# A transformer block on one core: the last product of the first attention moves into the second attention, some copies change their issuing queue, and the last output product is computed transposed

## The chip, the cores and the metric

The kernel runs on one core of a Trainium2 chip. TensorE multiplies matrices and transposes by multiplying with an identity, VectorE and ScalarE work element by element, GpSimd (POOL in the profile) does elementwise work and gathers, and SyncE (SP) does nothing but issue transfers. Every engine works through its own instructions in the order in which they were written; semaphores order work between engines. The metric is the device time of one execution in microseconds, as the median of three runs.

## The reference

The input `x` has 8 batches of 128 rows and 512 columns, all in float32. The block computes

```
h   = einsum('bsi,boi->bso', x, L0_cond_weight[itok_B_3_7])
x   = x + attention_1(h) @ wo          # 32 heads of 16, causal, 8 key/value heads
a   = attention_2(x) @ Wo              # 32 heads of 128, 8 key/value heads, rmsnorm and rotation
                                       # of q and k, 512 cached keys per batch plus 128 own
out = x + ffn(a)                       # a @ kernel + bias + two low-rank products
```

In the second attention the product with `Wo` is a sum over the 8 key/value heads (each with 4 query heads), so the kernel may add up one head after the other.

## The kernel before, in words

The order of the instructions on each engine is the order in which the Python code emits them. There is no planner: `tc.manual_schedule()` keeps it.

**First part, 0 to about 241 us.** A loop over `k` runs through 16 half batches of the conditioned projection and the first attention. For each batch `out_proj1(b)` multiplies the attention's output `oT[b]` by `wo_sb` (eight passes of 128x512 on TensorE, L650), adds the loaded rows of `x` on VectorE (L654) and stores the sum as `x1_kept[b]` (L655). `flip_x1(b)` transposes that sum (four transposes, L483) and ScalarE copies it to `x1T[b]` (L659), which the second attention reads. For the last batch both calls stand after the loop, around `own_keys(0)` and the last two `merge_w` (L468), so that the first scores of the second attention follow them on TensorE. Weights for the second attention are loaded during the loop, the ones of the output product by `load_wo(0)` and `load_wo(1)` (L135).

**Second part, about 241 to 1421 us.** `units` lists 64 pairs (head group `g`, batch `b`), with the two heads of a pair next to each other; a cached block holds both heads' keys. The loop over `u` is a software pipeline. Step `u` computes the scores and the softmax of unit `u`, the projections of unit `u + 1` (`q_matmul` L175, `kv_matmul` L215, `kv_turn`, `norms`, `queries` L252, `own_keys` L271), and the values and the output product of unit `u - 1` (`values` L894, `out_proj` L913). TensorE's order in a step is: scores with the next unit's q products between them, k and v products, values of the last unit, transposes of the next unit's q, output product of the last unit, transpose of the next unit's keys (kTp).

Within `scores`, VectorE masks and scales each of four score tiles (L851), ScalarE takes the exponential (L861) and later divides by the sum (L829), whose reciprocal VectorE makes (L828). VectorE transposes the four tiles in 32x32 blocks into `flips` (L832). Then 16 copies of 80 KB put the blocks in place as `pT` (L882), all issued by SyncE:

```
for a in range(4):
    for k in range(4):
        nc.sync.dma_start(out=s["pT"][32 * k : 32 * k + 32, a]..., in_=s["flips"][32 * a : 32 * a + 32, k]...)
```

Cached keys are turned in the same way, for two units at once: `turn_keys(n)` transposes blocks on VectorE into `flk` (L789) and `move_keys(n, a)` issues four copies each for `a` = 0 to 3 (L802). For most pairs eight of these fall into each step. The first such pair, n = 1, has to do all sixteen in step 1, and they stand in `pair_keys`, which `scores` calls after the third tile, ahead of the fourth exponential. The keys of units 0 and 1 are transposed by TensorE instead (`keys`, L263).

GpSimd adds the two halves of the rotation (L201), computes the power -1/2 for the norms (L242), and then gathers the cached rows (L158).

**The end.** Batch `b` is finished when its unit of the last head group has been added to `y_acc[b]` (L920). One step later `ffn_flip(b)` transposes it (L926) and ScalarE copies it as `yT` (L928); `ffn_lora(b)` makes a small product (axp, L945) which ScalarE copies to `ax`; `ffn(b)` makes the large products (fp, L960 and L961), adds the residual on VectorE (L963) and stores. In step 63 this is done for batch 6: flip, values of unit 62, axp, output product of unit 62, fp. Step 64 has only the values and the output product of unit 63, and step 65 the FFN of batch 7.

Of the kernel before, what the change touches and what calls it, by code (L numbers as in the profile page):

```python
# [41 lines left out]
def block_kernel(  # L42
# [75 lines left out]
    x1_kept = [dram.tile([P, DM], F32, tag=f"x1_{b}", name=f"x1_kept_{b}") for b in range(B)]  # L118
    b_kept = dram.tile([B, RANK, DM], F32, tag="b_eff", name="b_kept")
    res = {}  # L120

    weights = {}

# [8 lines left out]
    def load_wo(g):  # L132
        wo = wpool.tile([P, REP, DM], F32, tag="wo", name=f"wo_{g}")
        e = slice(g * REP * D2, (g + 1) * REP * D2)
        nc.sync.dma_start(out=wo[:], in_=wo2[e, :].rearrange("(r p) o -> p r o", p=P))  # L135
        weights[g].append(wo)
# [139 lines left out]
    with (  # L276
# [3 lines left out]
        wq_sb = p1w.tile([P, KC, REP * P], F32, tag="wq_sb", name="wq_sb")  # L280
        wk_sb = p1w.tile([P, KC, P], F32, tag="wk_sb", name="wk_sb")
        wv_sb = p1w.tile([P, KC, P], F32, tag="wv_sb", name="wv_sb")
        wo_sb = p1w.tile([P, REP, DM], F32, tag="wo_sb", name="wo_sb")
        xss, cws = {}, {}

        def load_x(b):
# [339 lines left out]
        def values1(k):  # L626
            b, hb = divmod(k, 2)
            h = H[k]
            if hb == 0:
                oT[b] = p1.tile([P, REP, S], F32, tag="oT1", name=f"oT1_{b}")  # L630
            ps = p_mm.tile([P, 2 * S], F32, tag="mm", name=f"o1_{k}")
            for half in range(2):
                for j in range(4):
                    nc.tensor.matmul(  # L634
                        ps[32 * j : 32 * j + 32, :],
                        vpad[b % 2][:, j, half].rearrange("p s d -> p (s d)"),
                        h[f"pT_{j}"][:, half, :],
                        start=(half == 0),
                        stop=(half == 1),
                    )  # L640
            nc.vector.tensor_copy(
                oT[b][:, 2 * hb : 2 * hb + 2, :].rearrange("p r t -> p (r t)"), ps[:]
            )
# [13 lines left out]
        def flip_x1(b):  # L657
            tp = transposed(x1[b], f"x1Tp_{b}")
            nc.scalar.copy(x1T[b][:], tp[:])  # L659
# [13 lines left out]
        for k in range(2 * B + 1):  # L673
            b, hb = divmod(k, 2)
            more, now, last = b + 1 < B, k < 2 * B, k - 1
            if now:
                scores1(k)
            if hb == 0:
                if b >= 2:
                    flip_x1(b - 2)  # L680
                if now:
                    exps1(k, 0)
                if more:
                    condition(b + 1)
                if k == 2 * B - 2:
                    for i in range(KC):
                        merge_a(i)
                if now:
                    exps1(k, 1)
                if k == 2 * B:  # L690
                    queries(0)
                if k:
                    flip_p(last, 0, by_vector)
                    flip_p(last, 1, by_vector)
                if now:
                    divide1(k, 0)
                    divide1(k, 1)
                if more:
                    kv = project_kv(b + 1)
                if k == 2 * B:  # L700
                    merge_b(0)
                if k:
                    flip_p(last, 2, by_scalar)
                    flip_p(last, 3, by_scalar)
                if more:
                    keep_k(b + 1, kv)
                if k == 2 * B:
                    merge_b(1)
                    for i in range(2):
                        merge_w(i)  # L710
                if k:
                    values1(last)
                if more:
                    keep_v(b + 1, kv)
                gather_w(b + 3)
                if k == 2 * B - 4:
                    merge_gates()
            else:
                if b >= 1:
                    out_proj1(b - 1)  # L720
                exps1(k, 0)
                exps1(k, 1)
                flip_p(last, 0, by_vector)
                flip_p(last, 1, by_vector)
                divide1(k, 0)
                divide1(k, 1)
                if more:
                    ps = project_q(b + 1)
                    keep_q(b + 1, ps)
                else:  # L730
                    for c in range(KC):
                        q_matmul(0, c)
                    for part in q_turn(0):
                        part()
                    for c in range(KC):
                        kv_matmul(0, c)
                flip_p(last, 2, by_scalar)
                flip_p(last, 3, by_vector)
                if not more:
                    kv_turn(0)  # L740
                    norms(0)
                if b + 2 < B:
                    flip_x(b + 2)
                values1(last)
                load_x(b + 4)
                if b == 0:
                    indices()
                elif b == 1:
                    tables(0)
                    load_qkv(0)  # L750
                    load_wo(0)
                elif b == 2:
                    tables(1)
                    nc.gpsimd.memset(minus_half[:], -0.5)
                elif b == 3:
                    load_qkv(1)
                    load_wo(1)
                elif b == B - 2:
                    gather(0, "kg")
                    gather(0, "vg")  # L760
                if b == 4:
                    merge_loads()
        keys(0)
        out_proj1(B - 1)
        own_keys(0)
        for i in range(2, KC):
            merge_w(i)
        flip_x1(B - 1)


    p2c = ctx.enter_context(tc.tile_pool(name="p2c", bufs=1))
# [7 lines left out]
    nc.gpsimd.memset(place[:, NBLK * P :], -3.0e38)  # L779

    y_acc = [p2c.tile([P, DM], F32, tag=f"y_{b}", name=f"y_{b}") for b in range(B)]

    def turn_keys(n):

# [13 lines left out]

    def move_keys(n, a):

        for b in range(4):
            nc.sync.dma_start(  # L802
                out=pairs[n]["kT"][32 * b : 32 * b + 32, :, a].rearrange("p c m i -> p c (m i)"),
                in_=pairs[n]["flk"][32 * a : 32 * a + 32, b].rearrange("p c m i -> p c (m i)"),
            )
# [9 lines left out]
    def scores(u, between, after):  # L815
# [62 lines left out]

        s["pT"] = p2.tile([P, 4, NBLK + 1, REP, 32], F32, tag="pT2", name=f"pT_{u}")
        for a in range(4):  # L880
            for k in range(4):
                nc.sync.dma_start(  # L882
                    out=s["pT"][32 * k : 32 * k + 32, a].rearrange("i c r j -> i (c r j)"),
                    in_=s["flips"][32 * a : 32 * a + 32, k].rearrange("i c r j -> i (c r j)"),
                )
# [21 lines left out]
    def out_proj(u, r):  # L907
        g, b = units[u]
        s = st[u]
        if r == 0:  # L910
            s["yp"] = p_mm.tile([P, DM], F32, tag="mm", name=f"yp_{u}")
        yp = s["yp"]
        nc.tensor.matmul(  # L913
            yp[:], s["oT"][:, r, :], weights[g][2][:, r, :], start=(r == 0), stop=(r == REP - 1)
        )
        if r == REP - 1:
            if g == 0:
                nc.scalar.copy(y_acc[b][:], yp[:])
            else:
                nc.vector.tensor_tensor(y_acc[b][:], yp[:], y_acc[b][:], ALU.add)  # L920


    def ffn_flip(b):
        tp = p_tp.tile([P, KC, S], F32, tag="tp", name=f"yTp_{b}")
        for c in range(KC):
            nc.tensor.transpose(tp[:, c, :], y_acc[b][:, c * P : (c + 1) * P], ident[:])  # L926
        yT = tile_a([P, KC, S], f"yT_{b}")
        nc.scalar.copy(yT[:], tp[:])  # L928
        return yT
# [35 lines left out]

    pending = []
    first = (NKV // 2 - 1) * 2 * B
    for u in range(N + 3):


        now, nxt, last = u < N, u + 1 < N, 1 <= u <= N
# [11 lines left out]
        if nxt:  # L983
# [2 lines left out]
            kv_turn(u + 1)  # L986
            after[1]()
        flipped = [(b, ffn_flip(b)) for b in pending]
        if last:
            values(u - 1)  # L990
        if nxt:
            norms(u + 1)
            queries(u + 1)
            keys(u + 1)
            if u > 2 and u % 2 and u // 2 + 2 < N // 2:
                turn_keys(u // 2 + 2)

            if u < 2:
                gather(u + 1, "kg")
            elif u % 2 == 0:  # L1000
                gather(u // 2 + 2, "kg")
            if u % 2:
                gather(u // 2 + 1, "vg")
        flipped = [(b, yT, ffn_lora(b, yT)) for b, yT in flipped]
        if last:
            for r in range(REP):
                out_proj(u - 1, r)
        if nxt:
            own_keys(u + 1)

        for n in range(2):
            g = (u + 1 - n) // (2 * B) * 2 + 2 + n
# [8 lines left out]
                ffn_loads(b + 1)  # L1021
        if u == first:
            ffn_loads(0)
        pending = [units[u - 1][1]] if last and units[u - 1][0] == NKV - 1 else []


# [76 lines left out]
```

## Time and profile before

| | |
|---|---|
| median of three runs | 1442.05 us (1441.12 to 1443.71) |
| the profiled execution, its own time | 1443.16 us |
| its span, first to last instruction | 1441.4 us |
| TensorE busy in the span | 1404.8 us (97%) |
| VectorE, ScalarE, GpSimd busy | 932.7 us, 652.6 us, 564.3 us |
| mean granted TensorE clock | 0.996 |
| SyncE's copies of pT, of kT | 1024 of 80 KB, 496 of 32 KB |

The profile shows one execution. PE stands for TensorE's multiplications, PEld for its weight loads, DVE for VectorE, ACT for ScalarE, POOL for GpSimd, SP for SyncE; a q after the name is the engine's sequencer, where transfers are issued. A name such as `pT<-fl` says which tile is written from which. In the timeline a line gives start and length in us, engine, source line, operation, shapes and count, and in brackets how long the engine was idle before and what ended the wait. Times count from the start of the span. A matmul of float32 appears as two passes, each with its own record.

### The profile page before, as it was taken

Reading aid. Unit: us, or ns where it says so; the run is one execution under the profiler, and the core shown is the slowest. Engines: PE = TensorE matmul, PEld = TensorE weight load, DVE = VectorE, ACT = ScalarE, POOL = GpSimd, SP = SyncE. Lnnn points to the kernel's source line nnn. Section 1 sums busy time; section 2 is a strip of 40 time slices with the busy share of each in tenths; the row PEclk is TensorE's granted clock in tenths of the full one; section 3 lists DMA queues with packets and bytes.
Section 4 is the critical chain, followed back from the end, with each engine's and each line's share of the span. In section 5 each row is a group of like instructions: output and inputs, shape, how many; then the busy total and the mean of one; then the engine's idle time right before and its main releaser. Section 6 shows DMA issues by size and latency. Waiting matters only on the chain.

```text
span 1441.4 us, 19823 instructions
## 1 busy us (share of the span) xinstructions
PE 1404.8 (97%) x5984; PEld 897.3 (62%) x6000; DVE 932.7 (65%) x2271; ACT 652.6 (45%) x1513; POOL 564.3 (39%) x546
## 2 busy tenths in 40 slices
PE   6999999899999999999999999999999999999997
PEld 5677764566666666666666666666666665666554
DVE  4666674666666666666666666666666665666652
ACT  3454543444444444444444444444444444344430
POOL 4675242433333333333433344444343333343220
PEclk9999999999999999999999999999999999999999
DMA  5233410444444575444445654444457544444442
GB/s 202 75 117 120 142 44 23 134 120 118 117 117 117 150 191 159 118 117 117 118 119 160 194 149 119 119 119 119 119 161 193 157 125 136 123 115 114 112 111 66
DMA packets 159770, 181.82 MB, mean 126 GB/s; under 512 B 94960, under 2 KB 100336, under 8 KB 159664
## 3 DMA queue, kind: packets, MB, share of 16 engines
q1 hardware_dynamic: 144816, 138.59, 34.1%
q0 software_dynamic: 14848, 41.96, 10.4%
q8 instruction: 49, 0.80, 0.2%
q14 instruction: 57, 0.47, 0.1%
HBM read 75.57 MB, written 4.72 MB: 56 GB/s over the span
## 4 chain that ended last, share of the span: by engine, by line
PE 92%; SPq 2%; DMA 2%; DVE 2%; issue 1%; ACT 1%; POOL 0%; DVEq 0%; POOLq 0%
PE op L894 18%; PE qp L175 15%; PE sc L838 15%; PE yp L913 15%; PE kvp L215 7%; PE sc L845 4%; PE hp L498 2%; PE att L650 2%; PE qTp L252 2%; PE qp L512 2%; PE fp L960 2%; PE pT1p L615 2%; PE o L634 2%; SPq L882 1%; PE sc L572 1%; PE sc L562 1%
## 5 line engine op out<-in xcount | busy, mean ns | idle before, releaser
L851 DVE CUSTOM_DVE_ANT_0 pr<-sc,mask,nq 128x640 f32<-128x640 f32 x256 | 225.8, 883 | 142.2 <-PE sc L845 130.1
L861 ACT ACTIVATE pr<-pr,nm 128x640 f32<-128x640 f32 x256 | 211.8, 827 | 188.8 <-DVE nm L851 185.9
L838 PE MATMUL sc<-kT,qT 128*128 128x512 f32 x512 | 263.8, 597 | 2.2 <-DMA pT<-fl 1.8
L175 PE MATMUL qp<-wq,x1T 128*128 128x512 f32 x512 | 251.2, 593 | 0.0
L894 PE MATMUL op<-pT,vg 128*128 128x256 f32 x1024 | 243.4, 381 | 4.7 <-DMA pT<-fl 4.3
L913 PE MATMUL yp<-wo,oT 128*128 128x512 f32 x512 | 231.0, 594 | 0.0
L201 POOL TENSOR_TENSOR qa<-qa,qb 128x512 f32<-128x512 f32 x64 | 81.6, 1276 | 371.9 <-DVE sums L828 371.9
L894 PEld LDWEIGHTS op<-pT,vg 128*128 128x128 f32 x1024 | 194.7, 191 | 32.4 <-issue 4.1
L829 ACT ACTIVATE pr<-pr,sums 128x640 f32<-128x640 f32 x256 | 208.4, 814 | 0.0
L832 DVE STREAM_TRANSPOSE fl<-pr 128x640 f32<-128x640 f32 x256 | 192.2, 807 | 0.8 <-DMA kT<-flk 0.6
L845 PEld LDWEIGHTS sc<-kTo,qT 128*128 128x128 f32 x512 | 97.0, 190 | 125.3 <-issue 104.4
L913 PEld LDWEIGHTS yp<-wo,oT 128*128 128x128 f32 x512 | 92.3, 190 | 93.3 <-issue 91.8
L158 POOL DMA_INDIRECT kg<-in_k_cache_dram,idx_kv x128 | 132.1, 1032 | 35.3 <-issue 34.9
L158 POOL DMA_INDIRECT vg<-in_v_cache_dram,idx_kv x128 | 128.2, 1002 | 36.7 <-issue 33.9
L838 PEld LDWEIGHTS sc<-kT,qT 128*128 128x128 f32 x512 | 88.1, 192 | 82.2 <-issue 78.6
L254 ACT COPY qT<-qTp 128x512 f32<-128x512 f32 x64 | 37.5, 586 | 205.8 <-PE qTp L252 205.8
L215 PEld LDWEIGHTS kvp<-wkv,x1T 128*128 128x128 f32 x512 | 97.3, 190 | 40.5 <-issue 30.1
L215 PE MATMUL kvp<-wkv,x1T 128*128 128x256 f32 x512 | 120.9, 379 | 0.0
L242 POOL TENSOR_TENSOR rs<-ss,minus_half 128x5 f32<-128x5 f32 x64 | 76.6, 1197 | 82.3 <-DVE ss L240 82.3
L175 PEld LDWEIGHTS qp<-wq,x1T 128*128 128x128 f32 x512 | 82.8, 191 | 31.5 <-issue 31.5
L845 PE MATMUL sc<-kTo,qT 128*128 128x128 f32 x512 | 99.3, 276 | 0.0
L606 POOL TENSOR_TENSOR pr<-pr,sums 128x1024 f32<-128x1024 f32 x32 | 60.0, 1898 | 92.6 <-DVE sums L605 89.7
(134 smaller groups left out, 1645.6 us busy)
## 6 DMA issues: line engine op xcount, KB each, us to landing
pT<-fl SPq DMA_DIRECT2D x1024, 80.0 KB
kT<-flk SPq DMA_DIRECT2D x496, 32.0 KB
wq<-in_wq_dram SPq DMA_DIRECT2D x8, 1024.0 KB
wo<-in_wo_dram SPq DMA_DIRECT2D x8, 1024.0 KB
wkv<-in_wkv_dram SPq DMA_DIRECT2D x8, 512.0 KB
xs<-in_x_dram SPq DMA_DIRECT2D x8, 256.0 KB
x_kept<-x SPq DMA_DIRECT2D x8, 256.0 KB
kg<-in_k_cache_dram,idx_kv POOLq DMA_INDIRECT x128, 3.6
```

The source lines that it names most:

```text
L158: nc.gpsimd.indirect_dma_start(out=dst[:, c].rearrange("p n d -> p (n d)"), out_offset=None, in_=src, in_offset=bass.IndirectOffsetOnAxis( ...
L175: nc.tensor.matmul(s["qp"][:].rearrange("p h d -> p (h d)"), x1T[b][:, c, :], weights[g][0][:, c, :], start=(c == 0), stop=(c == KC - 1),)
L201: nc.gpsimd.tensor_tensor(qa[:], qa[:], qb[:], ALU.add)
L215: nc.tensor.matmul(s["kp"][:], x1T[b][:, c, :], weights[g][1][:, c, :], start=(c == 0), stop=(c == KC - 1))
L829: nc.scalar.activation(prs[r][:], prs[r][:], AF.Copy, scale=sums[:, r : r + 1])
L832: nc.vector.transpose(s["flips"][:, :, :, r, :].rearrange("p b c j -> p c b j"), prs[r][:])
L838: nc.tensor.matmul(sc[:, : NBLK * P].rearrange("p (k j) -> p k j", j=32), s["qT"][:, r, :], s["kT"], start=True, stop=True,)
L845: nc.tensor.matmul(sc[:, NBLK * P : NK], s["qT"][:, r, :], s["kTo"][:], start=True, stop=True)
L851: nc.vector.tensor_tensor_reduce(out=pr[:], in0=sc[:, :NK], in1=mask[:], scale=s["nq"][:, r : r + 1], scalar=3.0e38, op0=ALU.add, op1=ALU.min,
L861: nc.scalar.activation(pr[:], pr[:], AF.Exp, bias=nm[:, r : r + 1], scale=-1.0, accum_out=sums[:, r : r + 1],)
L894: nc.tensor.matmul(ops[h][:, : 2 * S], cached(u, "vg", c) if c < NBLK else s["vo"][:], s["pT"][:, :, c, 2 * h : 2 * h + 2, :].rearrange("p ...
L913: nc.tensor.matmul(yp[:], s["oT"][:, r, :], weights[g][2][:, r, :], start=(r == 0), stop=(r == REP - 1))
```

## The change

It has four parts.

1. `out_proj1` and `flip_x1` of the last batch leave the first part. The attention's output of that batch is kept in `oT_kept`, a tile that outlives the first part, and `wo_sb` becomes the first tile in the pool of the second attention's output weights, which has two places. In step 0 of the second part, `out_proj_last` makes the product after the k and v products of unit 1 and before its norms, adds rows of `x` that are loaded again (`x_last`) and stores the sum; `flip_last` transposes it before `own_keys(1)`.
2. `load_wo(1)` has to wait for the place of `wo_sb` and moves to the end of step 0.
3. Eight of the sixteen copies `kT<-flk` of pair 1, and eight of the sixteen copies `pT<-fl` of units 62 and 63 each, are issued by ScalarE instead of SyncE. They stand in ScalarE's instructions where they stood in SyncE's.
4. The output product of unit 63 is computed transposed. `ffn_flip(7)` transposes the sum over all other units ahead of the values of unit 63, and `out_proj_turned` makes 16 blocks of 128x128 with weights and data exchanged, which VectorE adds to the transposed sum. The FFN of batch 7 follows in the same step, and the loop has two steps fewer.

```diff
+    oT_kept = one([P, REP, S], F32, "oT_kept")
...
-        wo_sb = p1w.tile([P, REP, DM], F32, tag="wo_sb", name="wo_sb")
+        wo_sb = wpool.tile([P, REP, DM], F32, tag="wo", name="wo_sb")
...
-                oT[b] = p1.tile([P, REP, S], F32, tag="oT1", name=f"oT1_{b}")
+                oT[b] = p1.tile([P, REP, S], F32, tag="oT1", name=f"oT1_{b}") if b + 1 < B else oT_kept
...
                     load_qkv(1)
-                    load_wo(1)
...
         keys(0)
-        out_proj1(B - 1)
         own_keys(0)
         for i in range(2, KC):
             merge_w(i)
-        flip_x1(B - 1)
...
+    x_last = p2c.tile([P, DM], F32, tag="res", name="x_last")
+    nc.sync.dma_start(out=x_last[:], in_=x[B - 1])
+
+    def out_proj_last():
+        ps = p_mm.tile([P, DM], F32, tag="mm", name="att1_last")
+        for r in range(REP):
+            nc.tensor.matmul(
+                ps[:], oT_kept[:, r, :], wo_sb[:, r, :], start=(r == 0), stop=(r == REP - 1)
+            )
+        x1 = tile_a([P, DM], "x1_last")
+        nc.vector.tensor_tensor(x1[:], ps[:], x_last[:], ALU.add)
+        nc.sync.dma_start(out=x1_kept[B - 1][:], in_=x1[:])
+        return x1
+
+    def flip_last(x1):
+        tp = p_tp.tile([P, KC, S], F32, tag="tp", name="x1Tp_last")
+        for c in range(KC):
+            nc.tensor.transpose(tp[:, c, :], x1[:, c * P : (c + 1) * P], ident[:])
+        nc.scalar.copy(x1T[B - 1][:], tp[:])
...
     def move_keys(n, a):
+        queue = nc.scalar if n == 1 and a > 1 else nc.sync
         for b in range(4):
-            nc.sync.dma_start(
+            queue.dma_start(
...
         for a in range(4):
+            queue = nc.scalar if u >= N - 2 and a > 1 else nc.sync
             for k in range(4):
-                nc.sync.dma_start(
+                queue.dma_start(
...
+    def out_proj_turned(u, before):
+        g, b = units[u]
+        yp = p_mm.tile([P, KC, S], F32, tag="mm", name=f"yp_{u}")
+        for c in range(KC):
+            for r in range(REP):
+                nc.tensor.matmul(
+                    yp[:, c, :],
+                    weights[g][2][:, r, c * P : (c + 1) * P],
+                    st[u]["oT"][:, r, :],
+                    start=(r == 0),
+                    stop=(r == REP - 1),
+                )
+        nc.vector.tensor_tensor(before[:], yp[:], before[:], ALU.add)
...
-    for u in range(N + 3):
+    for u in range(N + 1):
...
         flipped = [(b, ffn_flip(b)) for b in pending]
+        if u == N:
+            flipped.append((B - 1, ffn_flip(B - 1)))
         if last:
             values(u - 1)
+        if u == 0:
+            x1_last = out_proj_last()
         if nxt:
             norms(u + 1)
             queries(u + 1)
...
+        if u == N:
+            out_proj_turned(u - 1, flipped[-1][1])
         flipped = [(b, yT, ffn_lora(b, yT)) for b, yT in flipped]
-        if last:
+        if last and u < N:
             for r in range(REP):
                 out_proj(u - 1, r)
+        if u == 0:
+            flip_last(x1_last)
         if nxt:
             own_keys(u + 1)
+        if u == 0:
+            load_wo(1)
```

More of the change, by code (lines that the diff above doesn't have):

```diff
@@ L1023, in block_kernel @@
             ffn_loads(0)
-        pending = [units[u - 1][1]] if last and units[u - 1][0] == NKV - 1 else []
+        pending = [units[u - 1][1]] if last and u < N and units[u - 1][0] == NKV - 1 else []
 def kernel(
```

## The prediction

> **What bounds the kernel now.** I read the windows view first (us of the stretch, then busy us of PE, PEld, DVE, ACT, POOL, then granted clock, DMA share and GB/s), cut where the character of the work changes.
>
> ```profile
> 252.00:261.00 9.00, 5.53 (x17) 3.02 (x18) 4.60 (x13) 2.58 (x8) 5.36 (x7) 0.62 0.42 117
> ...
> 282.00:1118.00 836.00, 835.60 (x3051) 526.02 (x3050) 574.29 (x1496) 398.18 (x851) 331.67 (x331) 1.00 0.50 137
> ...
> 1400.00:1421.00 21.00, 16.72 (x63) 9.44 (x62) 9.02 (x20) 7.08 (x14) 0.00 (x0) 1.00 0.40 100
> 1421.00:1425.00 4.00, 4.00 (x12) 3.21 (x12) 0.06 (x1) 0.00 (x0) 1.26 (x1) 0.57 0.41 141
> ```
>
> For 836 us TensorE has no gap: there only fewer matmuls would help, and the change removes none. What can move lies in two places, the start of the second attention (252 to 289) and the last two steps (from 1393). The waits of PE in these two stretches name them (us in total, times, longest):
>
> ```profile
> PE kTp L271 <- DVE ka L245: 2.7, 1, 2.7
> PE sc L838 <- DMA pT<-fl: 1.8, 1, 1.8
> PE qTp L252 <- POOL qa L201: 1.1, 1, 1.1
> PE kgTp L263 <- ACT qT L254: 0.7, 1, 0.7
> ...
> PE op L894 <- DMA kT<-flk: 0.4, 1, 0.4
> ...
> PE op L894 <- DMA pT<-fl: 4.3, 2, 3.3
> ```
>
> The first step has nothing to fill 1.1 + 0.7 + 2.7 us, and the clock then drops. The waits on DMA are for copies that SyncE issues one at a time; the views by line give min/median/max ns of one issue:
>
> ```profile
> L882 SPq DMA_DIRECT2D pT<-fl x1024: 507/589/1933, 253.8 to 1418.6; - x171
> ...
> L802 SPq DMA_DIRECT2D kT<-flk x496: 585/600/1826, 265.5 to 1368.1; - x166
> ```
>
> Sixteen at 0.63 us from start to start are a queue of 10.1 us. The timeline of the end shows what it holds back, and two ScalarE instructions that will matter:
>
> ```profile
> 266.33 0.83 ACT L861 ACTIVATE pr<-pr,nm 128x640 f32<-128x640 f32 x1 [0.54 <-DVE nm L851]
> ...
> 1393.00 26.22 SPq L882 DMA_DIRECT2D pT<-fl  x32
> ...
> 1398.35 0.27 PE L271 MATMUL kTp<-ident,ka 128*128 128x128 f32 x1
> ...
> 1407.08 0.56 ACT L928 COPY yT<-yTp 128x512 f32<-128x512 f32 x1
> ...
> 1409.10 0.43 PE L945 MATMUL axp<-yT,a_eff 128*32 128x128 f32 x8
> ...
> 1420.83 3.22 PE L894 MATMUL op<-pT,vg 128*128 128x256 f32 x8 [3.31 <-DMA pT<-fl]
> ...
> 1431.29 0.66 PE L926 MATMUL yTp<-ident,y 128*128 128x128 f32 x4 [0.78 <-DVE y L920]
> 1431.98 0.59 ACT L928 COPY yT<-yTp 128x512 f32<-128x512 f32 x1 [22.12 <-PE yTp L926]
> 1432.62 0.43 PE L945 MATMUL axp<-yT,a_eff 128*32 128x128 f32 x8 [0.68 <-ACT yT L928]
> ```
>
> [...] 0.62 after the gaps of the first step, 0.57 after the 3.31 us. [...] ScalarE issues no DMA in this trace. [...]
>
> **A. The product and the flip moved into step 0.** Removed before the first scores: eight L650 matmuls at 0.43 us a slot (3.44) and four transposes (0.43), 3.9 us of TensorE. They come back in step 0 where TensorE idles 1.08 + 0.68 + 2.72 = 4.5 us, and where kTp to the first qp took 4.1 us at low clock against 2.05 one step later, another 2.0. Not all is filled: the new add (0.69 on VectorE, waiting for the product) stands ahead of norms(1), so rs (1.2, POOL) and ka come some 0.8 us later and kTp still waits about 1.5. Gain: 3.9 + 4.5 + 2.0 - 3.9 - 1.5 = **5.0 us** (3.5 if the clock still drops, 6.5 at most). The x_last load (issue 0.33) has 10 us until its add; a late landing would hold VectorE and then kTp. The x1 write and wo_1 load move behind SyncE's sixteen pT(0) copies and ahead of the kT copies: 0.35 + 0.5 us, in an idle gap of 0.86 (264.69 to 265.55). POOL's rs and the gathers behind it start 3.4 instead of 5 us earlier, worth at most 1 us on VectorE's flk, which has slack. wo_1 is used some 30 us after its issue. In its old place nothing waited for it, so leaving saves nothing there. All this is costed at nothing.
>
> **B. Eight kT copies of pair 1 on ScalarE.** SyncE's last kT goes out 5.1 us earlier; the 1.79 and, behind it in the queue, the 0.41 us wait can go: -2.2. But the eight stand in ScalarE's order ahead of the fourth exp of step 1 (266.33 above). They wait for VectorE's flk (ends 265.5). In the trace's records SyncE's copies take eight landing semaphores in turn, each waiting for the copy eight places before it. If ScalarE's go on in the same turn, each waits for the landing of a copy that SyncE has just issued: 2.5 us by my estimate, between 2.1 (the last pT issued at 1418.64, values at 1420.83, a little off for TensorE's start) and 3.4 (the last kT issued at 275.28, its scores at 278.66). ScalarE is then free at 265.5 + 2.6 + 8 x 0.64 = 273.3. The exp is 7.0 us late, so the reciprocal of its sum on VectorE (268.16) 6.2 us, and the four transposes, kb and oT behind it too; TensorE, in order, meets oT at its yp product 5.6 us late (0.6 of slack) and runs about 3.4 us at half clock (+1.7). Sum 7.3 - 2.2 = **+5.1**.
>
> **C. Half the pT copies of units 62 and 63 on ScalarE.** Unit 62: they wait for the transposes until 1393.0, the first landing is +2.1, eight issues 5.0: ScalarE is free at 1400.2 instead of going on at 1391.3. Behind it stand the square and vo of unit 63, then on the way to kTp the norm on VectorE (0.16), rs (1.2) and the two scalings: kTp starts at 1402.6 instead of 1398.35. That is +4.25, +1.7 for the clock, -0.96 since pT(62) no longer waits: +5.0. Unit 63: the transposes end near 1414.5 (was 1409.15); held 2.1 + 5.0, ScalarE copies yT of batch 6 at 1421.7, and axp, in order on TensorE ahead of a product and an FFN, starts at 1422.3 instead of 1409.10. From axp to the FFN's end 8.4, clock 1.7, flip 0.45, values 4.3: 1437.2.
>
> **D. The turned product.** 32 passes of 128x128 cost the same as 8 of 512 (the 32 passes of qp L512 take 3.6 us), but c = 0 needs both halves of oT: +0.25. After it: one add (0.2 + 0.69) instead of add, transposes, ScalarE copy (1431.29 to 1432.62): -1.33, since the flip of the partial sum stands in front of values. So 1437.2 + 3.85 + 0.9 + 0.35 puts fp at 1442.3, and the last add 4.67 us later at 1446.9, against 1437.64: C and D together **+9.3**.
>
> **Sum:** -5.0 + 5.1 + 9.3 = +9.4. The profiled execution was 1443.16 us (span 1441.4 and 1.76 around it), 1.1 above the median 1442.05; from the median the likeliest is **1451.5 us**. Its own range, 1446 to 1456, is the clock penalty at one or all of three places and A between its ends.
>
> **Rivals.** What the trace does not show is what a copy costs ScalarE: from nothing visible (it only queues) to 0.63 plus a landing; I take the upper value, because SyncE's issues are plainly serial and the order of the instructions is written out.
> *ScalarE hardly held* (the other side; point of decision: a hold of about 0.6 us a copy with no landing wait). Then A -5.0, B -2.2, and at the end: 0.96 less; values(63) at 1417.0, when TensorE is free, rather than 1420.83; no low clock (4.3 instead of 6.2); D -1.1: together -6.6. Sum -13.8: 1428.2. [...] Against it: ScalarE's instructions behind the copies are in program order.
> *Held by issue alone*, 0.63 us each without landing waits: B +2.4, C and D +4.0, A -5.0: +1.4; at 0.5 us each, -3.5. About 1442, 1438 to 1446.
> [...]
> *The change is void in A* because the product waits for something else: A is 0 and the rest as above, 1456.
>
> **Chances.** Held with landing waits 0.53 (slower); issue alone 0.15 (0.05 faster, 0.06 same, 0.04 slower); hardly held 0.28 (faster, 1427 to 1437); longer holds or A void 0.04 (slower). A measurement of this kernel tells 0.2%, 2.9 us, from no change. Faster 0.33, same 0.06, slower 0.61. The range runs from 1429, which leaves out nearly half of the fast case, to 1456.
>
> **What would show it.** A: no PE gap over 2 us near 250, first scores near 236.5. B: ScalarE idle 7 us before the fourth exp of step 1, PE idle before yp. C: yT of batch 6 right behind ScalarE's last DMA issue and axp idle for some 8 us. If ScalarE's DMA rows take 0.1 us, or later ScalarE work runs between them, I am wrong, and values(63) comes without a wait.

## The result and the profile after

The changed kernel took 1452.74 us (median of six runs, 1452.23 to 1453.57) against 1441.53 us for the kernel before in the same comparison (six runs): a ratio of 1.0076, 95% interval 1.0063 to 1.0089. It is slower by 0.8%. The profiled execution has a span of 1451.2 us, 9.8 more than before, and a mean clock of 0.993.

The waits of PE in the changed kernel (us in total, times, longest):

```profile
PE axp L984 <- ACT yT L967: 6.9, 1, 6.9
PE yp L937 <- DVE oT L926: 5.5, 1, 5.5
PE op L918 <- DVE sums L850: 5.0, 1, 5.0
...
PE qTp L254 <- POOL qa L203: 1.6, 1, 1.6
...
PE kTp L273 <- DVE ka L247: 1.1, 1, 1.1
```

No wait is put down to a copy of kT or pT any more, and most of the 2.7 us wait at kTp is gone. In their place stand three longer ones, one for each place where ScalarE issues copies. The windows (us, busy us of PE, PEld, DVE, ACT, POOL, clock, DMA share, GB/s) show that the clock drops at each of the three, and that the long middle is what it was:

```profile
265.00:273.00 8.00, 6.28 (x16) 5.08 (x17) 4.64 (x10) 3.25 (x8) 0.46 (x1) 0.57 0.78 208
282.00:1118.00 836.00, 836.00 (x3054) 526.43 (x3053) 575.33 (x1497) 398.08 (x852) 333.44 (x333) 1.00 0.50 137
1399.00:1406.00 7.00, 5.93 (x7) 2.53 (x8) 1.78 (x7) 0.00 (x0) 1.66 (x2) 0.51 0.02 4
...
1420.00:1427.00 7.00, 3.94 (x13) 1.76 (x14) 0.00 (x0) 0.85 (x2) 0.00 (x0) 0.54 0.55 135
```

The timeline of the start:

```profile
235.89 1.12 PE L860 MATMUL sc<-kT,qT 128*128 128x512 f32 x2
...
245.48 3.60 PE L789 MATMUL att_last<-wo_sb,oT_kept 128*128 128x512 f32 x8
...
248.33 16.27 SPq L906 DMA_DIRECT2D pT<-fl  x16
...
251.91 0.30 PE L273 MATMUL kTp<-ident,ka 128*128 128x128 f32 x1 [1.06 <-DVE ka L247]
...
259.83 5.70 ACTq L824 DMA_DIRECT2D kT<-flk  x8
265.58 0.83 ACT L883 ACTIVATE pr<-pr,nm 128x640 f32<-128x640 f32 x1 [6.66 <-DMA kT<-flk]
...
266.72 3.75 PE L918 MATMUL op<-pT,vg 128*128 128x256 f32 x8 [5.02 <-DVE sums L850]
...
271.36 0.42 DVE L926 COPY oT<-op 128x256 f32<-128x256 f32 x1 [0.41 <-PE op L918]
```

and of SyncE's pT(0) copies before:

```profile
253.78 10.91 SPq L882 DMA_DIRECT2D pT<-fl  x16
```

The clock record of the trace has 0.50 for 6.83 us at each of the three: from 265.88, from 1399.11 and from 1419.59. This is what "half clock" means below. The product fills the first step without a gap of its own, and full clock holds there (1.00 from 244 to 265). ScalarE's eight issues take 5.70 us, and the exponential behind them starts 0.05 us after the last one ends. But TensorE does not wait where I had put the wait, at yp. It waits earlier, at values(0), the product of unit 0's probabilities with its cached values, which reads pT(0). The rows of SyncE say why: its sixteen pT(0) copies, which took 10.91 us before, now last 16.27 us, up to 264.60. In the records of this trace each of these copies has one of eight landing semaphores, on which its arrival is counted, and the rows of SyncE and ScalarE name the same eight. Thirteen pT(0) copies have gone out by 257.15. The last three go out at 261.87, 262.56 and 264.09: each waits for the semaphore that it has in common with a kT copy of ScalarE (issued at 259.83, 260.60 and 261.90), and goes out 0.01 to 0.02 us after that one has landed (261.86, 262.54 and 264.07). The last of the three lands at 266.07, and TensorE's wait for it ends at 266.10. The releaser in the row, VectorE's last reciprocal, is inferred from the time; in e5_hold below that reciprocal is late too, and the values don't wait.

And the end, with TensorE's yp of unit 61 before and then the changed kernel:

```profile
1394.91 3.60 PE L913 MATMUL yp<-wo,oT 128*128 128x512 f32 x8
```

```profile
1392.54 4.97 SPq L906 DMA_DIRECT2D pT<-fl  x8
1392.55 5.33 ACTq L906 DMA_DIRECT2D pT<-fl  x8
...
1397.98 0.28 ACT L227 ACTIVATE junk<-kvp 128x128 f32<-128x128 f32 x1 [7.05 <-DMA pT<-fl]
...
1398.54 0.29 DVE L232 TENSOR_TENSOR ka<-kvp,ca 128x128 f32<-128x128 f32 x1 [6.02 <-ACT vo L229]
...
1400.07 6.60 PE L937 MATMUL yp<-wo,oT 128*128 128x512 f32 x8 [5.45 <-DVE oT L926]
...
1417.35 5.03 ACTq L906 DMA_DIRECT2D pT<-fl  x8
1422.42 0.59 ACT L967 COPY yT<-yTp 128x512 f32<-128x512 f32 x1 [7.09 <-DMA pT<-fl]
1423.06 0.66 PE L984 MATMUL axp<-yT,a_eff 128*32 128x128 f32 x8 [6.93 <-ACT yT L967]
...
1433.27 1.89 PE L918 MATMUL op<-pT,vg 128*128 128x256 f32 x8
```

Both queues issue side by side, eight copies in 5 us. ScalarE goes on only when its eight are issued; then come the square and vo of unit 63, VectorE's ka behind vo, oT behind ka, and TensorE's yp of unit 61, which takes 6.60 instead of 3.60 us at half clock. In step 63 yT of batch 6 follows the last issue by 0.04 us, and axp follows yT.

For the ledger I count from marks that every kernel has: TensorE's first kgTp, where the first part ends, and the start of its k and v products of units 2, 3, 5 and 63. The runs below come from three chips on which the kernel before took 1449 to 1451 us, not 1441.53, and the first part of every kernel 5 to 8 us longer. So a ratio is always to the kernel before in the same comparison, and places are given in us from the first kgTp, the last column in us from the products of unit 63. A ratio rests on all executions of a run, a place on the one that was profiled. The two can differ: of e5_hold the profiled execution took 4.3 us more than the median.

| kernel | ratio to before | to unit 2 | to unit 3 | to unit 5 | from unit 63 to the end |
|---|---|---|---|---|---|
| before | 1 | 32.55 | 52.36 | 88.72 | 52.93 |
| after | 1.0076 | 26.52 | 52.66 | 88.50 | 63.21 |
| e1_product | 0.9976 | 26.52 | 50.03 | 85.74 | 52.86 |
| e2_product_turn | 0.9975 | 26.52 | 50.23 | 85.95 | 52.09 |
| e3_keys | 1.0052 | 32.28 | 56.61 | 94.74 | 52.94 |
| e4_probs | 1.0075 | 32.97 | 52.82 | 89.29 | 63.76 |
| e5_hold | 1.0006 | 26.52 | 53.33 | 91.72 | 53.44 |
| e6_late_probs | 0.9939 | 26.52 | 49.89 | 85.60 | 47.28 |
| e7_keys_after_qt | 0.9935 | 26.52 | 45.70 | 87.77 | 47.29 |
| e9_keys_after_vo | 0.9958 | 26.52 | 53.78 | 89.49 | 47.29 |
| e10_keys_only | 0.9919 | 26.52 | 48.56 | 84.28 | 47.29 |
| e8_yt_vector | 1.0043 | 26.52 | 51.78 | 92.00 | 58.74 |

The 9.8 us of the two spans are: first part -0.85 (233.29 against 234.14), start -0.22, middle +0.61, end +10.28.

### The profile page after: what moved, and what is told of

The parts are those of the page before. It is cut to its first block, busy times and chain, and to the rows that moved or that the text cites. A ratio compares the mean times of both kernels' runs of the same rounds, so it can differ in the third digit from the quotient of the medians.

```text
span 1451.2 us, 19899 instructions
## 1 busy us (share of the span) xinstructions
PE 1409.7 (97%) x6024; PEld 900.5 (62%) x6024; DVE 933.3 (64%) x2271; ACT 652.4 (45%) x1513; POOL 564.1 (39%) x546
## 3 DMA queue, kind: packets, MB, share of 16 engines
q0 software_dynamic: 14848, 41.96, 10.2%
## 4 chain that ended last, share of the span: by engine, by line
PE 92%; DVE 2%; DMA 2%; issue 1%; ACT 1%; POOL 1%; ACTq 1%; SPq 0%; DVEq 0%; POOLq 0%
PE op L918 18%; PE yp L937 15%; PE qp L177 15%; PE sc L860 15%; PE kvp L217 7%; PE sc L867 4%; PE hp L500 2%; PE fp L999 2%; PE qTp L254 2%; PE att L652 2%; PE qp L514 2%; PE pT1p L617 2%; PE o L636 2%; PE sc L574 1%; PE sc L564 1%
```

## The experiments

### The parts, one at a time

**e1_product**: only the product and the flip moved (parts 1 and 2); all copies on SyncE, no turned product.

```diff
-        queue = nc.scalar if n == 1 and a > 1 else nc.sync
+        queue = nc.sync
...
-            queue = nc.scalar if u >= N - 2 and a > 1 else nc.sync
+            queue = nc.sync
...
```

> Parts 1 and 2 alone: the moved product and flip and the late wo_1 load; every copy is issued by SyncE and the last output product is as before. Theory (the move fills the idle time of step 0): in the changed kernel the q products of step 1 start 6.9 us earlier than before (254.2 against 261.1), and here SyncE's queue of sixteen kT copies then keeps TensorE waiting 2 to 3 us at the scores of step 2 instead of 1.8. Net 5 to 7 us faster than before, about 1435.5 us. Rival (the moved product only changes places and the key copies take the gain back): the wait at the scores of step 2 grows to 5 us or more and the time is within 2 us of before.

Measured: 0.9976 (0.9968 to 0.9984), 3.5 us faster, between what the two theories said. TensorE is 6.0 us ahead at unit 2, but only 3.0 at unit 5. The waits of PE say what is late next:

```profile
PE sc L860 <- DMA kT<-flk: 3.4, 1, 3.4
PE op L918 <- DMA pT<-fl: 3.2, 1, 3.2
```

The first is SyncE's queue: sixteen kT copies can't start before flk is there and take 10 us, so the scores of unit 2, now due earlier, wait longer than the 1.8 us before, and TensorE then runs at half clock for 3.4 us (the second of these products takes 1.92 us instead of 1.02). (The second is the old wait of unit 63.) Part 1 is a gain, and half of it is eaten by a queue that it doesn't touch.

**e2_product_turn**: the same with the turned last product (part 4), so that only ScalarE's copies are missing from the changed kernel.

> Parts 1, 2 and 4: everything but the copies issued by ScalarE. Theory (the ScalarE copies are the whole loss): about 1 us faster than the run with parts 1 and 2 alone, some 1434.5 us, since the turned product drops an add-transposes-copy of 1.3 us and adds a quarter of a us. Rival (the turned product costs more than it saves[...]): 1 us or more slower than the run with parts 1 and 2 alone.

Measured: 0.9975 (0.9966 to 0.9984). The end is 0.8 us shorter by the marks (52.09 against 52.86); by the ratios the two can't be told apart. The turned product shows no cost, and by the marks it saves 0.8 us.

**e3_keys**: the kernel before with the eight kT copies on ScalarE, nothing else (its lines after the edit stand one further down).

```diff
+        queue = nc.scalar if n == 1 and a > 1 else nc.sync
         for b in range(4):
-            nc.sync.dma_start(
+            queue.dma_start(
```

> The kernel before with only the eight kT copies of pair 1 on ScalarE. Theory H (ScalarE is held while it issues): its fourth exp of step 1 comes 5 to 6 us late, TensorE waits about 3.5 us for oT ahead of the yp product and runs some us at half clock, while 2.2 us of waiting for copies go: 2 to 4 us slower than before. Theory L (landing semaphores shared by SyncE's and ScalarE's copies): TensorE waits 4 to 5 us at values of unit 0, because SyncE's last pT(0) copies stand behind ScalarE's copies; 5 to 6 us slower. A third (the changed kernel lost nothing here): 2 us faster.

Measured: 1.0052 (1.0039 to 1.0065), 7.5 us slower, more than either theory had set; +4.3 us at unit 3, +6.0 at unit 5. Its timeline:

```profile
270.65 5.50 ACTq L803 DMA_DIRECT2D kT<-flk  x8
...
277.19 3.75 PE L895 MATMUL op<-pT,vg 128*128 128x256 f32 x8 [3.51 <-DMA kT<-flk]
```

TensorE waits at values(0), where theory L had put the wait, and for a DMA. In the records of the semaphores, SyncE's thirteenth pT(0) copy goes out at 268.26 and the last three at 273.35, 273.99 and 274.68: each waits for a landing semaphore (three of the same eight) that a kT copy of ScalarE has taken at 271.41 to 272.71, and those copies stand behind the first, which had waited for flk until 270.65. Although these kT copies stand later in the code, they hold the three semaphores first in this run. This gave a second theory, *shared semaphores*, beside *hold*: not what stands behind the copies in ScalarE is late, but what SyncE has yet to issue. (Since a semaphore serves many copies, 204 or 205 of SyncE's in the kernel before, the bracket of a row can name another copy than the one that is waited for: values(0) reads pT, scores read kT.)

**e4_probs**: the kernel before with the sixteen pT copies of units 62 and 63 on ScalarE, nothing else.

```diff
+            queue = nc.scalar if u >= N - 2 and a > 1 else nc.sync
             for k in range(4):
-                nc.sync.dma_start(
+                queue.dma_start(
```

> The kernel before with only the sixteen pT copies of units 62 and 63 on ScalarE, the last output product as before. Theory H (held): VectorE waits for ScalarE's vo ahead of oT of unit 61, so TensorE waits about 5.5 us before the yp product of step 62, and about 7 us before axp of batch 6, with two stretches of 6.8 us at half clock: 10 to 12 us slower than before. Rival (only one of the two places is on the chain, the other hides in the wait for pT): 4 to 6 us slower.

Measured: 1.0075 (1.0062 to 1.0088), end +10.8 us. PE waits 5.5 us at yp and 7.1 at axp, as in the changed kernel. So these copies alone make the whole loss of the end, as theory H said.

### Hold or semaphores in step 1

**e5_hold**: e2_product_turn with eleven plain ScalarE copies where the kT issues stood.

```diff
+            if u == 1:
+                hold = p2c.tile([P, DM], F32, tag="res", name="hold")
+                for _ in range(11):
+                    nc.scalar.activation(hold[:], pairs[1]["flk"][:]...[:, :DM], AF.Copy)
```

> Product moved and last product turned, all copies on SyncE; in place of ScalarE's kT copies in step 1 stand 11 plain ScalarE copies of 512 values of flk into a spare tile (about 5.5 us of ScalarE, output not used). It holds ScalarE as long as the eight DMA issues did, but takes no landing semaphore. Theory 'hold': the fourth exp of step 1 is some 5 us late, VectorE's four transposes and oT(0) after it, and TensorE waits 4 to 5 us at yp L937, with a half-clock stretch behind it; the 3.5 us wait for kT (SyncE's queue, not moved) is swallowed by that delay. Net against the kernel with the same two parts and no hold (ratio to the kernel before 0.9975): +1 to +2 us, ratio 0.9982 to 0.9990. Theory 'shared semaphores' says of this run only that values(0) does not wait and that SyncE's pT(0) copies run through without a gap: its own +5 us wait is absent. If the hold were harmless: ratio 0.9975 and no wait at yp.

Measured: 1.0006 (0.9997 to 1.0014). The eleven took 7.24 us, more than I had set:

```profile
268.57 7.24 ACT L839 ACTIVATE hold<-flk 128x512 f32<-128x512 f32 x11 [1.30 <-DVE flk L809]
275.72 0.81 ACT L891 ACTIVATE pr<-pr,nm 128x640 f32<-128x640 f32 x1
...
281.47 5.65 PE L945 MATMUL yp<-wo,oT 128*128 128x512 f32 x8 [6.66 <-DVE oT L934]
```

Values(0) doesn't wait; TensorE stands 6.66 us at yp, with half clock behind it (yp takes 5.65 us instead of 3.60). The chain of the prediction exists, at its place, and its wait of 6.66 us fits the hold of 7.24. The whole costs more than the +1 to +2 us expected: by the ratios 4.5 us against e2_product_turn. Up to unit 3 it is 3.1 us, net of the wait for kT that it swallows (53.33 against 50.23), and at the end 1.4, where the half clock lasts twice as long in this execution (6.8 us). Another 2.7 are lost in step 2 of the profiled execution, where VectorE stands still (see the last section); this execution is slower than the run's median, so the others need not have that loss.

**e9_keys_after_vo** turns it round: kT copies on ScalarE where they hold up nothing urgent. All sixteen are written behind vo of unit 2, and four of them are issued by ScalarE (S stands for SyncE, A for ScalarE). The sixteen pT(1) copies are written behind kTo of unit 2, four of them for ScalarE, and the late pT copies of e6_late_probs (below) are in it as well.

```diff
             kv_turn(u + 1)
+            if u == 1:
+                move_keys_early("SSSSSSASASASASSS")
...
```

> As e7_keys_after_qt, but the four kT copies stand one instruction earlier in ScalarE's order, behind vo of unit 2, where ScalarE is idle too. There they take landing semaphores that the first kT copies of SyncE need as well. Theory 'hold': ScalarE has a gap of 2.4 us there and qT is not due before 278.4, so this is as fast as e7_keys_after_qt or faster (ratio 0.989 to 0.992). Theory 'shared landing semaphores': SyncE's first kT copy cannot go out at 268.5 but waits until the first copy of ScalarE has landed, about 274; its queue ends 5 us later, TensorE's wait for kT becomes 5 to 6 us and is followed by half clock: ratio 0.9945 to 0.997, 4 to 7 us slower than e7_keys_after_qt.

Measured: 0.9958 (0.9944 to 0.9971). Its timeline:

```profile
267.03 0.40 SPq L137 DMA_DIRECT2D wo<-in_wo_dram  x1
...
269.18 0.74 ACTq L836 DMA_DIRECT2D kT<-flk  x1
269.22 0.57 ACT L204 ACTIVATE sq<-qp 128x512 f32<-128x512 f32 x1
...
271.26 0.61 ACTq L836 DMA_DIRECT2D kT<-flk  x1
...
272.80 7.78 SPq L836 DMA_DIRECT2D kT<-flk  x12
...
284.26 2.05 PE L872 MATMUL sc<-kT,qT 128*128 128x512 f32 x2 [7.02 <-DMA pT<-fl]
```

SyncE is free at 267.4 and issues nothing for 5.4 us: its first kT copy needs the semaphore of ScalarE's first, which lands at 272.74. The scores of unit 2 wait 7.02 us, more than the 5 to 6 expected; the ratio is where the theory of shared semaphores had put it. No instruction of ScalarE was late on TensorE's path. So the shared semaphore alone stopped SyncE for 5.4 us here, without any hold.

**e7_keys_after_qt**: the same one instruction later in ScalarE's order, behind qT of unit 2, and with the four further back among the sixteen. There they take other semaphores, and SyncE's kT copies follow its load of wo by 0.1 us.

```diff
             queries(u + 1)
+            if u == 1:
+                move_keys_early("SSSSSSSSASASASAS")
...
```

> As e6_late_probs, and in step 1 four of the sixteen kT copies of pair 1 issued by ScalarE behind the qT copy of unit 2 (a gap of some 3 us in ScalarE's work), four of the pT(1) copies behind kTo of unit 2. Expected: TensorE's wait for kT (3.5 us) falls to about 1, its half clock goes: -2.5 to -4.5 us against e6_late_probs, ratio 0.990 to 0.992. Were it true that any kT copy on ScalarE costs a hold or a landing wait, it would be no faster than e6_late_probs.

Measured: 0.9935 (0.9921 to 0.9948), 8.1 us earlier than e9_keys_after_vo at unit 3 (45.70 against 53.78) and 4.2 earlier than e6_late_probs, as expected. But at unit 5 it is 2.2 us behind e6_late_probs: the gain is given back in step 2, and the ratio is that of e6_late_probs (0.9939), not the 0.990 to 0.992 expected.

```profile
285.79 0.94 POOL L160 DMA_INDIRECT vg<-in_v_cache_dram,idx_kv  x1 [0.30 <-issue]
...
289.38 0.88 DVE L885 CUSTOM_DVE_ANT_0 pr<-sc,mask,nq 128x640 f32<-128x640 f32 x1 [6.31 <-PE kvp L217]
...
290.76 1.97 PE L937 MATMUL op<-pT,vg 128*128 128x256 f32 x8 [1.66 <-DMA pT<-fl]
```

VectorE stands 6.31 us ahead of the third scores of unit 2, though TensorE had finished those by 283.7. And the pT(1) copies, shared with ScalarE, are late: SyncE's twelve took 10.20 us (12 x 0.63 = 7.6 without waits).

**e10_keys_only**: as e7_keys_after_qt, with the sixteen pT(1) copies on SyncE again.

> As e7_keys_after_qt, with the sixteen pT(1) copies back on SyncE: only four kT copies of pair 1 on ScalarE behind qT of unit 2, and the late pT copies of units 62 and 63. If e7 gave its 4.3 us back because pT(1) was shared (three landing waits in SyncE's queue, 10.2 us for twelve copies), SyncE now ends pT(1) at about 287.6, values(1) waits 1 us or less, and this is 3 to 4 us faster than e6_late_probs (ratio 0.9939): 0.991 to 0.992. If the 6.3 us in which VectorE stood before the third scores of unit 2 in e7 have another cause, they come again and the ratio is 0.993 to 0.994.

Measured: 0.9919 (0.9906 to 0.9932), 1438.00 us against 1449.88. The ratio is as expected. The long stop of VectorE did not come, and values(1) didn't wait; but since the stop also came in a run that leaves pT(1) on SyncE (e8_yt_vector), this does not show what causes it. TensorE, however, now waits 2.1 us for kT, where e7_keys_after_qt waited 0.5; up to unit 5 it is 1.3 us ahead of e6_late_probs, by the ratios 2.9, not 3 to 4. It is the fastest of all, faster than both kernels; whether it beats e6_late_probs is unclear, since the intervals overlap.

### The end: what stands behind the copies

**e6_late_probs**: e2_product_turn with ScalarE's pT copies back, but behind work that is due earlier: for unit 62 four copies (not eight) after qT of unit 63, for unit 63 eight after ax of batch 6. The other copies of the two units are written at the same places, for SyncE.

```diff
             queries(u + 1)
+            if u == N - 2:
+                move_probs(u, "SSSSSASASASASSSS")
...
         flipped = [(b, yT, ffn_lora(b, yT)) for b, yT in flipped]
+        if u == N - 1:
+            move_probs(u, "SA" * 8)
...
```

> Product moved and last product turned; ScalarE issues pT copies of units 62 and 63 as in the changed kernel, but behind work of its own that is due earlier: of unit 62 four copies after the qT copy of unit 63, of unit 63 eight copies after ax of batch 6. Theory 'ScalarE is held 0.6 us a copy, and what stands behind it decides': nothing urgent stands behind them now, so the two waits for pT at the end (1.1 and 2.8 us) and the half-clock stretch after the second (1.7) go and no wait at yp or axp takes their place: -5 to -5.6 us against the kernel with the same two parts and SyncE alone, ratio to the kernel before 0.9936 to 0.9945. Rival 'DMA issue by ScalarE is itself slow, or two queues land no sooner than one': ratio stays 0.9975 or above.

Measured: 0.9939 (0.9925 to 0.9952), the end 4.8 us shorter than with SyncE alone (47.28 against 52.09).

```profile
1400.40 2.77 ACTq L913 DMA_DIRECT2D pT<-fl  x4
1403.56 0.27 ACT L275 COPY kTo<-kTp 128x128 f32<-128x128 f32 x1 [2.90 <-DMA pT<-fl]
...
1414.09 5.62 ACTq L913 DMA_DIRECT2D pT<-fl  x8
...
1422.69 1.89 PE L925 MATMUL op<-pT,vg 128*128 128x256 f32 x8
```

The issues cost about what they cost in the changed kernel (0.7 us a copy here). Nothing on TensorE's path waits for ScalarE behind them, and values(63) starts without a wait at full clock. The one new wait is 1.2 us at yp of unit 62.

**e8_yt_vector**: the changed kernel with the copy of batch 6's yT on VectorE.

```diff
-        nc.scalar.copy(yT[:], tp[:])
+        if b == B - 2:
+            nc.vector.tensor_copy(yT[:], tp[:])
+        else:
+            nc.scalar.copy(yT[:], tp[:])
```

> The changed kernel with one instruction moved: the copy of batch 6's yT from PSUM is made by VectorE (behind the four transposes of unit 63) and not by ScalarE, so it no longer stands behind ScalarE's eight pT(63) copies. Theory 'in the last step the loss is what stands behind the copies, that is yT of batch 6 and with it axp': yT comes at about 1418 and not 1422.4 (on the time of the changed kernel's trace), TensorE's wait at axp falls from 6.9 to about 2 us, the half clock behind it shortens or goes, pT(63) has landed in time: -4.5 to -7 us against the changed kernel (ratio to before 1.0076), ratio 1.003 to 1.0045. Rival 'the last step is slow for another reason (turned product, SyncE, landings)': the wait moves to values(63) and the ratio stays at 1.006 or above.

Measured: 1.0043 (1.0026 to 1.0060), the end 4.5 us shorter than in the changed kernel (58.74 against 63.21).

```profile
1426.00 0.65 DVE L968 COPY yT<-yTp 128x512 f32<-128x512 f32 x1
1426.11 5.03 ACTq L906 DMA_DIRECT2D pT<-fl  x8
...
1426.70 0.43 PE L987 MATMUL axp<-yT,a_eff 128*32 128x128 f32 x8 [1.82 <-DVE yT L968]
```

ScalarE is held 5.03 us as before, but yT no longer stands behind it, and the wait at axp falls from 6.93 to 1.82 us, as the theory said.

## Why the prediction was right, and which of its steps were not

Forecast 1451.5 us, measured 1452.74. The mechanism, that ScalarE is held by the copies and that what stands behind them sets the end, is shown by e4_probs, e6_late_probs and e8_yt_vector. That the number came within 1.3 us is luck in part: the hold was shorter than forecast, the path and the half clock behind it longer, and A and B were not terms that can be added.

| step | forecast, us | measured by the marks, us |
|---|---|---|
| A, product into step 0 | -5.0 | -3.0 alone (-6.0 at unit 2) |
| B, kT copies | +5.1 | +2.6 on top of A and D (88.50 against 85.95), +6.0 alone (1.8 of it in step 2, where VectorE stood) |
| C and D | +9.3 | +10.3 (C alone +10.8, D -0.8) |
| sum | +9.4 | +9.8 of the profiled executions, +11.2 of the medians |

Along its own marks the changed kernel is 6.0 us ahead at unit 2 and 0.2 at unit 5: A and B together -0.2, forecast +0.1.

**A.** Filled gaps, kTp's 1.5 (1.06 measured), full clock: right, and at unit 2 even 1 us better. First scores at 235.89, forecast near 236.5. The step that failed is that I let the 5.0 us run through to the end as a term of its own. By my own working SyncE's kT queue ended 5 us earlier only through B; without B it is what is late next, for 3.4 us and a half-clock stretch (e1_product).

**The hold.** I set 2.1 to 2.6 us for a first landing plus 0.64 a copy. The copies cost 0.63 to 0.71 us each on the mean of eight, little more than SyncE's 0.63, but no landing wait came on top: in the records ScalarE's copies at the end took the odd and SyncE's the even ones of the eight semaphores, and the holds were 5.70, 5.33 and 5.03 us, not 7.1 to 7.7. In all three places ScalarE's next instruction starts 0.04 to 0.10 us after the end of its last issue (265.58, 1397.98 and 1422.42 after 265.53, 1397.88 and 1422.38). Here the rival *held by issue alone* was right and I was wrong.

**B.** The step that failed is the place. I had searched the queue of ScalarE for who stands behind the copies, and not the queue of SyncE for who needs their semaphores, though I had named the semaphores. The hold alone gives the forecast wait at yp (6.66 us after 7.2 of hold, e5_hold; forecast 5.6 after 7.0). In the changed kernel the values of unit 0 wait first, for SyncE's last three pT(0) copies. e9_keys_after_vo shows the shared semaphores stopping SyncE with no hold on the path. No run took away one of the two in the changed kernel itself, but its trace gives an estimate. Had values(0) run when due, at 261.7, TensorE would have come to yp at about 266.5 (4.3 us of values and 0.4 of qTp, as before). VectorE, behind the late exponential, is free for oT only at 270.96 and needs some 0.7 us for it: a wait of about 5 us at yp. So by this estimate the two waits lie side by side, each would have remained without the other, and TensorE pays once.

**C, unit 62.** ScalarE was free at 1397.98, not 1400.2: the hold was 5.33 us and not 7.1, and the kernel reached this place 0.5 us earlier. The path was wrong too: I followed the norm and kTp (4.25 us). VectorE's ka already waits for vo, and oT stands behind ka in VectorE's order (the rows above), so yp, which is ahead of kTp on TensorE, was 5.45 us late. And the clock term of 1.7 was 3.0 (yp 6.60 instead of 3.60 us): at this wait the half-clock stretch was 6.83 us long, not 3.41 as at the wait of 3.31 us in the kernel before. From the products of unit 63 to values(62): 7.49 us more (5.45 + 3.0 - 0.96), forecast 5.0. No run takes this path alone; it is read from the rows above and from e4_probs, where yp waits the same 5.5 us.

**C, unit 63, and D.** The transposes ended later than forecast, by unit 62's error, and the hold was shorter by 2.1: yT came at 1422.42, forecast 1421.7; axp at 1423.06, forecast 1422.3. Values(63) ran without a wait, as forecast. From values(63) to the end the kernel gained 2.6 us (17.91 against 20.53), forecast 3.0: 1.9 for the full clock and 1.1 for D. (I had read 6.2 us for these values before; they took 6.08.)

**Rivals.** *ScalarE hardly held* falls: no later work of ScalarE runs between the issues (idle for 6.66, 7.05 and 7.09 us in the changed kernel). An overlap shows in one direction only: in e9_keys_after_vo the square (269.22), the divide (269.69) and vo (270.66), written ahead of the copies, run while ScalarE's sequencer issues from 269.18 on; what is written behind the copies in the changed kernel waited for the last of them. *Longer holds* fall: SyncE and ScalarE took 4.97 and 5.33 us for eight copies each, at the same time. *Held by issue alone* had the right size of the hold, and with +1.4 a wrong sum: it shortened the hold and kept my short path and short half clock behind it. *Void in A* falls by e1_product.

## What to carry to other kernels

A copy on ScalarE's queue cost ScalarE the full issue time here, 0.63 to 0.71 us, so it belongs where nothing urgent stands behind it: the eight issues of unit 63, ahead of yT, made the stretch from values(62) to values(63) 5.4 us longer (21.62 against 16.21), and two ScalarE instructions later they were part of a gain of 4.8. Before moving a transfer, look at both queues: what stands behind it in the new one, and which later transfers of the old one share its landing semaphore (in e9_keys_after_vo that stopped SyncE for 5.4 us). And when a gap is filled, ask at once which transfer is late next, since part of the gain goes there.

## What the runs showed of the hardware that I had not expected

- **Length of the half-clock stretch.** In the second attention half clock lasted 6.8 us behind every wait of 5.0 to 7.1 us, and once 10.2 (e4_probs, at axp). A part of it can lie in the wait itself: in the changed kernel it begins 0.84 us before values(0), 0.96 before yp and 3.47 before axp. The wait of 5.45 us at yp so cost 3.0 us more (yp took 6.60 instead of 3.60). Behind waits of 1.8 to 3.6 us it lasted 3.4 us or did not come, and 6.8 in four places (the first step of the kernel before and of e4_probs; e3_keys behind 3.5 us; the end of e5_hold behind 2.8). The same wait can do either: behind 2.4 us at yp it came in e7_keys_after_qt and not in e5_hold. The shortest waits with half clock behind them were 2.1 us (e10_keys_only) and 1.8 (e8_yt_vector), both shorter than the 3.31 us of the kernel before; these runs don't show what decides it.
- **ScalarE issues ahead of itself.** Its DMA issue at 269.18 (e9_keys_after_vo) starts before instructions written earlier have run: the square starts at 269.22, vo at 270.66.
- **A stop of VectorE, not settled.** In step 2 VectorE stood 3.3 us (e3_keys), 4.6 (e5_hold), 6.3 (e7_keys_after_qt) and 3.7 (e8_yt_vector) ahead of a score tile that TensorE had finished 3.6 to 5.7 us before VectorE took it; in the other eight kernels there was no such stop. Step 2 is 2 to 6 us longer in these four than in e2_product_turn. The program alone does not make it: up to step 63 e8_yt_vector is the changed kernel, which shows none. Each stop ended 1.9 to 2.7 us after the end of POOL's last gather of vg. It also ended 0.02 to 0.03 us after a record of TensorE's semaphore, for which VectorE waits, and in the 7 to 11 us before that record all such records are missing (in e7_keys_after_qt from 278.75 to 289.36). In the ten experiments 240 to 259 of TensorE's 1093 to 1095 such records are missing, in the profiles of the two kernels none; a stretch without records stands in step 2 of nine of the ten, also where VectorE did not stop. Whether the semaphore came late, or the recording itself held the engines up, these traces can't tell. The places at unit 5 of these four runs carry the stop with them, so the ratios are the better measure there.
